# Vision tower: the tokenizer's first two layers as one product over raw pixels, q formed transposed and x (Wv W_out) joined to k in linear attention

## The chip, the cores and the metric

One core of a Trainium2 chip. The time is device microseconds from a run without the profiler, the median of three runs. The core has TensorE (PE, with weight loads PEld beside it), VectorE (DVE), ScalarE (ACT), GpSimd (POOL) and SyncE (SP), which issues most transfers. All data are float32.

## The reference

Four images of 3 x 224 x 224 are cut into 8 x 8 patches, 784 tokens of 192 pixel values for each image, and pass through two layers of a tower.

```python
# tokenizer
tokens = layernorm(patches, ln1_g, ln1_b)              # over 192
tokens = tokens @ W1 + b1                              # 192 -> 256
tokens = layernorm(tokens, ln2_g, ln2_b)
tokens = concatenate([tokens, tokens, tokens], axis=1) # three equal copies
h1 = silu(layernorm(tokens @ Wp1 + bp1, lnp_g, lnp_b))
return h1 @ Wp2 + bp2
```

```python
# linear attention of layer 1, on the normed rows x
q, k, v = split(x @ W_qkv + b_qkv, 3)
q = q - mean(q);  k = k - mean(k)                      # over the 256 channels
q2, k2 = q * q, k * k
k2 = l2_normalize(k2 / (sum(k2) + 1e-7), axis=-2)      # over the tokens
q2 = l2_normalize(q2 / (sum(q2) + 1e-7), axis=-1)      # over the channels
t2 = (q2 @ (k2.T @ v)) / sqrt(N)
return (v + t2) @ W_out + b_out
```

Between the two, layer 0 has attention over the four images (norm, q, k, v, a gate) and a mixture of six experts, of which each token takes two. After the linear attention layer 1 has a feed-forward of a shared part and four experts. Each part's result is added to the rows. The three copies of the tokens are equal, so the kernel computes one of them and writes each row of the result three times.

## The kernel before

Tokens are handled in tiles of 112 rows, 7 to an image, 28 in all; a group is four tiles. `h` (L258) holds all rows of the residual stream in SBUF. The stages, in order of time:

- Start. `img` (four transfers on SP and ACT, L211) has one image in 28 partitions, `W1`, `ln1` (the norm's scale and shift) and the rest follow. `turn_patches(k)` (L342) turns four patch columns at a time on PE into `pT`, pixels on partitions, and ACT copies them out (L352). `bn_stats` of the pixels (L443) is on DVE. After five of seven column groups `first_layer` (L357) folds the norm's scale and the subtraction of the mean into `W1`, and puts the rows into the order of `pT` with `perm` (L390). `patch_scales` (L397) makes one factor per token (`rtok`). DVE and PE follow the order of the program here (`manual_schedule`).
- Tokenizer, three steps deep (`tokenize`, L499). For group g: `pw1`, 256 wide, over `pT` (L508), the factor and `b1` by DVE (L466), statistics (L470), root on ACT (L474), `xn` on DVE (L482). Then for group g-1: turn of `xn` (L297), scale and shift of the second norm on ACT (L492), `pwp1` with `Wp1` (L514), bias, statistics and `xn` again. Then for group g-2: turn, Silu on ACT (L492), `pwp2` (L522) and the bias into `h` (L461). A planner orders the instructions of each engine.
- Keys and values of layer 0 (`keys_values`, L1016), between the last two steps of the tokenizer and after them, in an order by hand. Keys of all images have to be there before the first image's attention ends.
- Attention of layer 0, routing, and the experts over 30 blocks of 256 rows, which are scattered to `xrows` and fetched from `yrows` with indirect DMAs on POOL (L901, L1369). Both arrays are filled with zeros at the start (L253). In the expert stage DVE and SP are ordered by hand; `centred_weights` (L577) takes the mean out of the columns of q and k in `Wqkv`.
- Linear attention, in eight units of four or three tiles (`units`, L1349; the loop is L1705). Per unit: `x_t` turns the normed rows, `q_k` (L1558) forms q and k, 512 wide, DVE adds the bias (L1578), ACT squares q, k and q again with sums (L1582, L1583), `scales` (L1591) scales both (L1606 on ACT, L1607 on DVE), `q_t` turns q (L1628). Per image `k_x` forms k^T x (L1648) and `kv_out` multiplies with Wv W_out, which `layer1_weights` (L593) made in unit 1. `rows_out` (L1682) adds x (Wv W_out) (L1689) and q kvo (L1694) in PSUM and DVE adds the sum to `h` (L1700). The rows of the experts of the unit after are added in `stats_one` (L1377), inside `q_k`. The planner orders all engines here.
- Feed-forward of layer 1 in seven groups, with its router `gate` (L1506).

PSUM has seven banks in turn (`ps_tile`) and one bank of its own for small products (`psum_s`, L70), one user at a time.

Of the kernel before, what the change touches and what calls it, by code (L numbers as in the profile page):

```python
# [27 lines left out]
P = 128  # L28
# [32 lines left out]
def tile_vit_tower(ctx: ExitStack, tc: tile.TileContext, a: dict, out: bass.AP):  # L61
# [45 lines left out]
    for n in (E0, E1):  # L107
# [4 lines left out]
    allones = const.tile([TT, TT], F32, tag="allones", name="allones")  # L112
# [3 lines left out]
        out=before, in_=allones, compare_op=ALU.is_ge, fill=0.0, base=-1,  # L116
# [36 lines left out]
    for key, name in (  # L153
        ("ln2_g", "L0_tok_ln2_g"), ("ln2_b", "L0_tok_ln2_b"), ("lnp_g", "L0_tok_lnp_g"),
        ("lnp_b", "L0_tok_lnp_b"), ("gamma", "L0_attn_gamma"), ("beta", "L0_attn_beta"),
        ("bg", "L0_attn_bg"), ("router_b1", "L0_ffn_router_b1"), ("sb1", "L1_ffn_sb1"),
        ("sb2", "L1_ffn_sb2"),
    ):
        want(key, a[name].rearrange("(r p) -> r p", p=P), a[name].shape[0] // P)
# [5 lines left out]
    nrows = sum(k for _, k, _ in plan)  # L165
    stage = const.tile([nrows, P], F32, tag="stage", name="stage")
# [37 lines left out]
    tok = ctx.enter_context(ExitStack())  # L204
    tokp = tok.enter_context(tc.tile_pool(name="tok", bufs=1))
    WID = HP * PATCH
    CY = CH * PATCH
    img = tokp.tile([TT, 32, WID], F32, tag="img", name="img")
    for b in range(NI):
        eng = nc.scalar if b % 2 else nc.sync  # L210
        eng.dma_start(  # L211
            out=img[b * HP : (b + 1) * HP, :CY, :].rearrange("h (c p) w -> h c (p w)", c=CH),
            in_=a["x"][b].rearrange("c (h p) w -> h c (p w)", p=PATCH),
        )
    ln1 = tokp.tile([2, PD], F32, tag="ln1", name="ln1")
    nc.scalar.dma_start(out=ln1[:1], in_=a["L0_tok_ln1_g"].unsqueeze(0))
    nc.scalar.dma_start(out=ln1[1:], in_=a["L0_tok_ln1_b"].unsqueeze(0))
    W1 = tokp.tile([KP, 2, D], F32, tag="W1", name="W1")
    nc.sync.dma_start(out=W1, in_=a["L0_tok_W1"].rearrange("(s p) n -> p s n", p=KP))
# [8 lines left out]
    b1 = spread(tokp, "b1", a["L0_tok_b1"])  # L228
    Wp1 = tokw.tile([P, 2, D], F32, tag="Wp1", name="Wp1", bufs=1)
    nc.sync.dma_start(out=Wp1, in_=a["L0_tok_Wp1"].rearrange("(c p) n -> p c n", p=P))  # L230
    bp1 = tokw.tile([TT, D], F32, tag="bp1", name="bp1", bufs=1)
    nc.gpsimd.dma_start(out=bp1, in_=a["L0_tok_bp1"].partition_broadcast(TT))
# [106 lines left out]

    pT = tokp.tile([P, 2, NI * HP, HP], F32, tag="pT", name="pT")  # L340

# [15 lines left out]
    def first_layer():  # L357

        gbT = tokp.tile([KP, 2, 2], F32, tag="gbT", name="gbT")
        pt = ps_tile("pgb")  # L360
        for i in range(2):
# [3 lines left out]
        nc.vector.tensor_copy(gbT.rearrange("p i k -> p (i k)"), pt[:KP, :4])  # L365
        bb = tokp.tile([KP, 2, TT], F32, tag="bb", name="bb")
        W1g = tokp.tile([KP, 2, D], F32, tag="W1g", name="W1g")
        for i in range(2):
            nc.vector.tensor_copy(bb[:, i, :], gbT[:, i, 1:2].to_broadcast([KP, TT]))
            nc.vector.tensor_scalar(  # L370
                W1g[:, i, :], W1[:, i, :], gbT[:, i, 0:1], None, ALU.mult
            )
        pw = ps_tile("pbw")[:TT, :D]
        for i in range(2):
            nc.tensor.matmul(pw, bb[:, i, :], W1[:, i, :], start=(i == 0), stop=(i == 1))
        pm = ps_tile("pw1m")[:KP, :D]
        for i in range(2):
            nc.tensor.matmul(
                pm, allones[:KP, :KP], W1g[:, i, :], start=(i == 0), stop=(i == 1)
            )  # L380
        nc.vector.tensor_tensor(b1, pw, b1, ALU.add)
        for i in range(2):
            nc.vector.scalar_tensor_tensor(
                W1g[:, i, :], pm, -1.0 / PD, W1g[:, i, :], ALU.mult, ALU.add
            )
        Wc = tokp.tile([P, 2, D], F32, tag="Wc", name="Wc")
        pp = ps_tile("pwc").rearrange("p (i d) -> p i d", i=2)
        for i in range(2):
            for half in range(2):
                nc.tensor.matmul(  # L390
                    pp[:, i, :], perm[:, half, i].rearrange("p g k -> p (g k)"),
                    W1g[:, half, :], start=(half == 0), stop=(half == 1),
                )
        nc.vector.tensor_copy(Wc, pp)
        return Wc

    def patch_scales(st):  # L397


        d = tokp.tile([TT, HP], F32, tag="pd", name="pd")  # L400
        v = tokp.tile([TT, HP], F32, tag="pv", name="pv")
# [4 lines left out]
        nc.scalar.activation(v, v, AF.Sqrt, bias=eps[:TT], scale=1.0 / PD)  # L406
        nc.vector.reciprocal(v, v)
# [3 lines left out]
            rr, v.unsqueeze(1).to_broadcast([TT, 4, HP]),  # L411
# [4 lines left out]
        rtok = tokp.tile([TT, NT], F32, tag="rtok", name="rtok")  # L416
        nc.vector.tensor_copy(rtok, pr)
        return rtok
# [4 lines left out]
    perm = tokp.tile([KP, 2, 2, 4, 32], F32, tag="perm", name="perm")  # L423
    pst = tokp.tile([TT, HP, 6], F32, tag="pst", name="pst")
    with tc.manual_schedule(engines={mybir.EngineType.DVE, mybir.EngineType.PE}):
        nc.vector.memset(perm, 0.0)
# [3 lines left out]
        for half in range(2):  # L430
            for i in range(2):
# [5 lines left out]
                )  # L437
        for k in range(HP // GT):
            if k == 5:
                W1g = first_layer()  # L440
            turn_patches(k)
            for w in range(k * GT, (k + 1) * GT):
                nc.vector.bn_stats(pst[:, w, :], img[:, :CY, w * PATCH : (w + 1) * PATCH])  # L443
        rtok = patch_scales(pst)
# [7 lines left out]
    def added(pm_of, dst, bias, stats, scale=None):  # L452

        st = mv = None
        if stats:
            st = small.tile([TT, GT, 6], F32, tag="st", name="st")
            mv = small.tile([TT, GT, 2], F32, tag="mv", name="mv")
        for two in halves(range(GT)):
            pm = pm_of(two)
            if scale is None:  # L460
                nc.vector.tensor_tensor(  # L461
                    dst[:, two[0] : two[0] + 2, :], pm, over(bias, 2), ALU.add
                )
            else:
                for i, j in enumerate(two):
                    nc.vector.scalar_tensor_tensor(  # L466
                        dst[:, j, :], pm[:, i, :], scale(j), bias, ALU.mult, ALU.add
                    )
            for j in two if stats else ():
                nc.vector.bn_stats(st[:, j, :], dst[:, j, :])  # L470
                nc.vector.bn_aggr(mv[:, j, :], st[:, j, :])
        if stats:
            r = small.tile([TT, GT], F32, tag="rstd", name="rstd")
            nc.scalar.activation(r, mv[:, :, 1], AF.Sqrt, bias=eps[:TT])  # L474
            return mv, r

    def rows_of(y, stats):
        mv, r = stats
# [9 lines left out]
    def turned_rows(xn, func, g, b):  # L488
        xT = tokw.tile([P, 2, GN], F32, tag=f"xT{g}", name=f"xT{g}")

        def put(c, pt):
            nc.scalar.activation(xT[:, c, :], pt, func, scale=col(g, c), bias=col(b, c))  # L492
# [4 lines left out]
    second, third = {}, {}  # L497

    def tokenize(g):  # L499
        if 1 <= g <= len(groups):  # L500
# [1351 lines left out]
```

## Time and profile before

| | us |
|---|---|
| time, three runs | 812.31, 815.91, 816.70 (median 815.91) |
| profiled execution | 849.85 |
| its span, first to last instruction | 848.1 |
| images landed, first patch statistics | 17.2 |
| first product of the tokenizer (L508) | 39.3 |
| second group of keys and values (L1016) starts turning | 150.4 |
| last product of the expert stage ends | about 517 |
| linear attention's last output row (L1694) ends | about 703 |

The profiled execution is one run under the profiler. Stretches of time below are in us from the start of its span. "PEclk" is the share of its full clock that TensorE was granted. A stage's limit is read from the engine that is busy there, not from shares of the whole span.

### The profile page before, as it was taken

The numbers are of one execution on the slowest core, as the hardware profiler recorded it, in microseconds if no ns is written. First come the engines' busy times: TensorE is split into PE (matmuls) and PEld (weight loads), VectorE is DVE, ScalarE is ACT, GpSimd is POOL, SyncE is SP. The second block draws the span as 40 slices with busy tenths as digits, with TensorE's granted clock in tenths as the row PEclk, the third lists the DMA queues.
The fourth block names the chain that finished last, engine by engine and source line by source line (L and its number), as shares of the span: only waits on it lengthen the run. The fifth ranks groups of instructions, "written<-read, shape, count | busy, mean of one in ns | idle before, by whom it ended". The sixth has DMA issues, their size and how long they took to land. (4 is left out here: it accounts for less than half of the span.)

```text
span 848.1 us, 11129 instructions
## 1 busy us (share of the span) xinstructions
PE 746.0 (88%) x3669; PEld 525.4 (62%) x3669; DVE 515.1 (61%) x1619; ACT 318.2 (38%) x758; POOL 129.3 (15%) x151
## 2 busy tenths in 40 slices
PE   2879988999788788799999999348999999999996
PEld 2758765555465466678878885335767675555553
DVE  4369886585787874346445655358995745544441
ACT  1333535455547573242222323323564612222221
POOL 5100000000024605430030022744000000000000
PEclk9999999999999988799999999759999999999999
DMA  8999990000001293332342224311000001333333
GB/s 197 360 421 419 419 384 0 1 0 1 1 22 55 82 367 95 103 127 75 100 131 88 94 88 137 93 52 55 1 2 0 1 3 27 100 101 101 99 100 100
DMA packets 58286, 97.52 MB, mean 115 GB/s; under 512 B 14590, under 2 KB 48564, under 8 KB 53364
## 3 DMA queue, kind: packets, MB, share of 16 engines
q1 hardware_dynamic: 51100, 80.78, 27.7%
q0 software_dynamic: 6224, 14.13, 5.8%
q10 hardware_dynamic: 904, 1.89, 0.9%
q8 instruction: 29, 0.48, 0.2%
q14 instruction: 29, 0.24, 0.1%
HBM read 31.04 MB, written 65.74 MB: 114 GB/s over the span
## 5 line engine op out<-in xcount | busy, mean ns | idle before, releaser
L901 POOL DMA_INDIRECT xrows<-xn,pos x56 | 59.9, 1070 | 282.4 <-ACT kq L665 233.2
L1369 POOL DMA_INDIRECT ys<-yrows,pos x56 | 54.3, 969 | 163.5 <-DMA yrows<-yb 134.0
L1173 PE MATMUL pb<-xTb,own 128*128 128x256 f32 x240 | 60.3, 396 | 7.0 <-DVE hb L1181 2.1
L1190 PE MATMUL pyb<-own,hb 128*128 128x256 f32 x240 | 59.4, 392 | 4.4 <-ACT hb L1179 4.4
L1173 PE MATMUL pb<-hb,own 128*128 128x256 f32 x240 | 58.8, 388 | 0.3 <-DVE hb L1181 0.3
L1179 ACT ACTIVATE hb<-pb,own 128x256 f32<-128x256 f32 x74 | 34.7, 473 | 61.7 <-PE pb L1173 42.1
L1173 PEld LDWEIGHTS pb<-xTb,own 128*128 128x128 f32 x240 | 45.5, 198 | 16.7 <-ACT xTb L1163 3.8
L1190 PEld LDWEIGHTS pyb<-own,hb 128*128 128x128 f32 x240 | 46.9, 197 | 12.0 <-ACT hb L1179 5.2
L297 PE MATMUL pt<-ident,xn 112*128 112x112 f32 x280 | 42.2, 281 | 12.4 <-DVE xn L482 6.9
L1574 PE MATMUL pqk<-Wqkv,lxT 128*112 128x512 f32 x112 | 50.0, 595 | 0.5 <-ACT lxT L81 0.5
L297 PEld LDWEIGHTS pt<-ident,xn 112*128 112x128 f32 x280 | 32.4, 148 | 26.4 <-issue 9.1
L1173 PEld LDWEIGHTS pb<-hb,own 128*128 128x128 f32 x240 | 44.5, 195 | 6.2 <-DVE hb L1181 0.7
L1196 DVE TENSOR_TENSOR yb<-pyb,eb 128x512 f32<-128x512 f32 x30 | 20.7, 691 | 45.5 <-PE pyb L1190 35.3
L306 PE MATMUL pe<-xT,eW 128*128 128x448 f32 x112 | 45.2, 546 | 0.0
L1648 PE MATMUL pukx<-xa,uk 112*128 112x258 f32 x112 | 29.0, 415 | 18.5 <-ACT uk L1606 18.5
L1163 ACT COPY xTb<-ptb 128x512 f32<-128x512 f32 x30 | 17.5, 583 | 73.8 <-PE ptb L1159 65.2
L1181 DVE TENSOR_SCALAR hb<-pb,own 128x256 f32<-128x256 f32 x46 | 22.2, 482 | 30.9 <-PE pb L1173 29.6
L1648 PEld LDWEIGHTS pukx<-xa,uk 112*128 112x128 f32 x112 | 22.7, 208 | 22.3 <-issue 18.8
L317 PE MATMUL pwo<-Wo,oT 128*112 128x256 f32 x112 | 29.0, 413 | 7.6 <-DVE oT L730 6.7
L1574 PEld LDWEIGHTS pqk<-Wqkv,lxT 128*112 128x112 f32 x112 | 19.2, 177 | 25.2 <-issue 22.7
L690 DVE SCALAR_TENSOR_TENSOR prod<-kq 128x784 f32<-128x784 f32 x32 | 30.4, 971 | 7.2 <-ACT kq L665 5.0
L1582 ACT ACTIVATE qk<-qk 112x256 f32<-112x256 f32 x56 | 22.8, 407 | 28.1 <-DVE qk L1578 23.8
(339 smaller groups left out, 1525.4 us busy)
## 6 DMA issues: line engine op xcount, KB each, us to landing
xrows<-nothing SPq DMA_DIRECT2D x19, 1024.0 KB
yrows<-nothing SPq DMA_DIRECT2D x19, 1024.0 KB
out_dram<-h SPq DMA_DIRECT2D x26, 336.0 KB
xb<-xrows SPq DMA_DIRECT2D x30, 256.0 KB
yrows<-yb SPq DMA_DIRECT2D x30, 256.0 KB
ew<-in_L_ffn_expert_w_dram SPq DMA_DIRECT2D x6, 768.0 KB
wb<-wd SPq DMA_DIRECT2D x28, 112.0 KB
img<-in_x_dram ACTq DMA_DIRECT2D x2, 588.0 KB
```

What stands on the lines that cost most here:

```text
L297: nc.tensor.transpose(pt[:, j * TT : (j + 1) * TT], xn[:, j, c * P : (c + 1) * P], ident[:TT, :TT])
L306: nc.tensor.matmul(pm[: wcols.stop - wcols.start, :n], w[:, c, wcols], xT(c), start=(c == 0), stop=(c == chunks - 1),)
L317: nc.tensor.matmul(pm[:, i, :], xT(c, t), w[:, c, :], start=(c == 0), stop=(c == chunks - 1))
L690: nc.vector.scalar_tensor_tensor(prod, qTs[s][:, o, :], 1.0, kT[:, o, t * SEQ : (t + 1) * SEQ], ALU.mult, ALU.mult, accum_out=atts[s][:, o ...
L901: put = nc.gpsimd.indirect_dma_start(out=xrows[:, :], out_offset=bass.IndirectOffsetOnAxis(ap=pos[:, k, t0 + j : t0 + j + 1], axis=0), in_ ...
L1173: nc.tensor.matmul(pm, wm[:, c, o * P : (o + 1) * P], src[:, c, :], start=(c == 0), stop=(c == 1),)
L1179: nc.scalar.activation(dst[:, o, :], pm, AF.Relu, bias=b)
L1190: nc.tensor.matmul(pm[:, t, :], src[:, c, t * P : (t + 1) * P], wm[:, c, :], start=(c == 0), stop=(c == 1),)
L1369: got = nc.gpsimd.indirect_dma_start(out=y[:, j, k, :], out_offset=None, in_=yrows[:, :], in_offset=bass.IndirectOffsetOnAxis(ap=pos[:, k, ...
L1574: nc.tensor.matmul(pqk, xT[:, c, cut(j, 1)], Wqkv[:, c, : 2 * D], start=(c == 0), stop=(c == 1),)
L1582: nc.scalar.activation(half, half, AF.Square, accum_out=ss[:, j, i : i + 1])
L1648: nc.tensor.matmul(pg, uks[u][:, k, c * P : (c + 1) * P], xas[u % 4][:, k, : D + 2], start=(j == 0), stop=(j == TPI - 1),)
```

## The change

- Start: the vectors, `W1` and `Wp1` are fetched ahead of the images; `b1` is one row instead of a copy per partition; `Wp1` and `bp1` move to the pool of the first stage. Row 24 of `img` in its last column now takes each patch's standard deviation (ACT's root, written in place), so that it is turned with the pixels and multiplies `b1` in the product.
- `first_layers` takes the place of `first_layer`, ahead of the first patches. It also folds the second norm's scale, shift and mean into `Wp1` and forms the product of both layers, so that `Wall` is 512 wide: the first layer's result in its first half (only its variance is used) and both layers' in the second.
- `first_rows` takes the place of the first two steps of the tokenizer: one 512-wide product per tile, statistics of its first half straight from PSUM, a copy of the second half by ACT, then factor, bias, statistics and `xn`. The turn between the layers and its activation go. The tokenizer is two steps deep.
- Linear attention: `q_of` forms q transposed (weights stationary), squares it on the way out of PSUM; the sums for its scale come from `norms`, with products of 32 columns and a turn in `psum_s`; the scale is applied in `rows_out`. `k_of` forms k and x (Wv W_out) in one 512-wide product, except in unit 0, and adds the latter to `h` at once; `rows_out` then has only q kvo. W_v in `Wqkv` is overwritten by Wv W_out. `layer1_weights` is called before unit 1.

```diff
+    nc.sync.dma_start(out=ln1[:1], in_=a["L0_tok_ln1_g"].unsqueeze(0))
+    nc.scalar.dma_start(out=ln2[:2], in_=a["L0_tok_ln2_g"].rearrange("(r p) -> r p", p=P))
+    nc.sync.dma_start(out=ln1[1:], in_=a["L0_tok_ln1_b"].unsqueeze(0))
+    nc.scalar.dma_start(out=ln2[2:], in_=a["L0_tok_ln2_b"].rearrange("(r p) -> r p", p=P))
+    nc.sync.dma_start(out=W1, in_=a["L0_tok_W1"].rearrange("(s p) n -> p s n", p=KP))
+    nc.scalar.dma_start(out=b1, in_=a["L0_tok_b1"].unsqueeze(0))
+    nc.scalar.dma_start(out=Wp1, in_=a["L0_tok_Wp1"].rearrange("(c p) n -> p c n", p=P))
     for b in range(NI):
         eng = nc.scalar if b % 2 else nc.sync
         eng.dma_start(
...
+    def without_mean(w, n, dim):
+        pm = ps_tile("pmean")[:n, :D]
+        for i in range(2):
+            nc.tensor.matmul(pm, allones[:n, :n], w[:, i, :], start=(i == 0), stop=(i == 1))
+        for i in range(2):
+            nc.vector.scalar_tensor_tensor(
+                w[:, i, :], pm, -1.0 / dim, w[:, i, :], ALU.mult, ALU.add
+            )
+    def first_layers():
...
+        for i in range(2):
+            nc.vector.tensor_scalar(W1g[:, i, :], W1[:, i, :], g1(i), None, ALU.mult)
+        without_mean(W1g, KP, PD)
...
+        nc.vector.tensor_tensor(b1, pw, b1, ALU.add)
...
+        nc.tensor.matmul(pp[:, 1, :], srow, b1, start=False, stop=True)
+        Wall = tokp.tile([P, 2, 2 * D], F32, tag="Wall", name="Wall")
+        nc.vector.tensor_copy(Wall[:, :, :D], pp)
+        for c in range(2):
+            nc.vector.tensor_scalar(W2[:, c, :], Wp1[:, c, :], g2(c), None, ALU.mult)
...
+        without_mean(W2, P, D)
...
+        nc.scalar.copy(WcT, pt)
...
+        nc.vector.tensor_tensor(bp1, pw, bp1, ALU.add)
+        pp = ps_tile("pw2").rearrange("p (i d) -> p i d", i=2)
+        for i in range(2):
+            for f in range(2):
+                nc.tensor.matmul(
+                    pp[:, i, :], WcT[:, f, i * P : (i + 1) * P], W2[:, f, :],
+                    start=(f == 0), stop=(f == 1),
+                )
+        nc.vector.tensor_copy(Wall[:, :, D:], pp)
+        return Wall
+    def patch_stds(k):
+        w0 = k * GT
+        for w in range(w0, w0 + GT):
+            nc.vector.bn_stats(pst[:, w, :], img[:, :CY, w * PATCH : (w + 1) * PATCH])
...
+        nc.vector.tensor_tensor(d, st[:, :, 1], st[:, :, 4], ALU.subtract)
+        nc.vector.tensor_tensor(v, st[:, :, 2], st[:, :, 5], ALU.add)
+        nc.vector.scalar_tensor_tensor(d, d, PD / 4.0, d, ALU.mult, ALU.mult)
+        nc.vector.tensor_tensor(v, v, d, ALU.add)
+        nc.scalar.activation(
+            img[:, CY, w0 * PATCH : (w0 + GT) * PATCH].rearrange("q (w x) -> q w x", x=PATCH)[
+                :, :, PATCH - 1
+            ],
+            v, AF.Sqrt, bias=eps[:TT], scale=1.0 / PD,
+        )
...
+        Wall = first_layers()
         for k in range(HP // GT):
-            if k == 5:
-                W1g = first_layer()
+            patch_stds(k)
             turn_patches(k)
...
+    def first_rows(g):
...
+        for j in range(GT):
+            pm = ps_tile("pw1")[:TT]
+            for c in range(2):
+                nc.tensor.matmul(
+                    pm, pTf[:, c, cut(t0 + j, 1)], Wall[:, c, :], start=(c == 0), stop=(c == 1)
+                )
+            nc.scalar.copy(y[:, j, :], pm[:, D:])
+            nc.vector.bn_stats(st[:, j, :], pm[:, :D])
+            nc.vector.bn_aggr(mv[:, j, :], st[:, j, :])
...
+        for j in range(GT):
+            nc.vector.scalar_tensor_tensor(
+                y[:, j, :], y[:, j, :], r[:, j : j + 1], bp1, ALU.mult, ALU.add
+            )
+            nc.vector.bn_stats(st[:, j, :], y[:, j, :])
+            nc.vector.bn_aggr(mv[:, j, :], st[:, j, :])
...
     def tokenize(g):
+        if g < len(groups):
+            normed[g] = first_rows(g)
         if 1 <= g <= len(groups):
+            third[g - 1] = turned_rows(normed.pop(g - 1))
...
+    def k_of(u):
...
+                if lw:
+                    pk = ps_tile("pk")[:TT]
+                    for c in range(2):
+                        nc.tensor.matmul(
+                            pk, xT[:, c, cut(j, 1)], Wqkv[:, c, D:], start=(c == 0), stop=(c == 1)
+                        )
+                    nc.vector.tensor_tensor(kr[:, j, :], pk[:, :D], bqkv[:, D : 2 * D], ALU.add)
+                    ht = h[:, b * TPI + j0 + j, :]
+                    nc.vector.tensor_tensor(ht, pk[:, D:], ht, ALU.add)
+                nc.scalar.activation(
+                    kr[:, j, :], kr[:, j, :], AF.Square, accum_out=ss[:, j : j + 1]
+                )
...
+    def q_of(u):
...
+        for o in range(2):
+            pq = mm_t(
+                n * TT, Wqkv, slice(o * P, (o + 1) * P), lambda c: xTs[u][:, c, : n * TT], "pq1"
+            )
+            nc.scalar.activation(qT[:, o, : n * TT], pq, AF.Square, bias=bq[:, o : o + 1])
+        nc.scalar.activation(q4[:, :, : n * TT], qT[:, :, : n * TT], AF.Square)
+    def norms(u):
...
+        for c in range(2):
+            for j in range(n):
+                nc.tensor.matmul(
+                    pg[32 * j : 32 * (j + 1), :], ones32, q4[:, c, cut(j, 1)],
+                    start=(c == 0), stop=(c == 1),
+                )
...
+        nc.scalar.copy(qn, pg)
+        pr = psum_s.tile([P, 512], F32, tag="pss", name="pqn")[:TT, :n]
+        nc.tensor.matmul(
+            pr, qn, ident.rearrange("p (j e) -> p j e", e=32)[: 32 * n, :n, 0],
+            start=True, stop=True,
+        )
...
     def rows_out(u):
...
+            pq = mm_rows(two, lambda c, j: qT[:, c, cut(j, 1)], kvo, "pqo")
+            for i, j in enumerate(two):
+                nc.vector.scalar_tensor_tensor(
+                    ht[:, i, :], pq[:, i, :], r[:, j : j + 1], ht[:, i, :], ALU.mult, ALU.add
+                )
...
+            k_of(0)
+            q_of(0)
             squares[0] = scales(0)
             fold(0, squares.pop(0))
+            lw.extend(layer1_weights(bvs))
+            Wvo, bvo = lw[:2]
...
         if u < len(units):
-            q_k(u, 0, 2)
+            k_of(u)
+            norms(u - 1)
```

## The prediction

> **What bounds the kernel now.** I read three views: the page (who is busy, when), busy time by stage, and the chain of work that ended last. First the page:
>
> ```profile
> span 848.1 us, 11129 instructions
> PE 746.0 (88%) x3669; PEld 525.4 (62%) x3669; DVE 515.1 (61%) x1619; ACT 318.2 (38%) x758; POOL 129.3 (15%) x151
> PE   2879988999788788799999999348999999999996
> DVE  4369886585787874346445655358995745544441
> PEclk9999999999999988799999999759999999999999
> DMA  8999990000001293332342224311000001333333
> ```
>
> One slice is 21.2 us. PE (TensorE) is full almost everywhere. It is not full at the start (slices 0 to 3) and in slices 25 and 26, where its clock falls too. DMA is full until 125 us, but with the zero fill of `xrows` and `yrows`, which nothing near it waits for. So I cut the two stages that the change touches:
>
> ```profile
> core 0: us, PE busy (x) PEld busy (x) DVE busy (x) ACT busy (x) POOL busy (x), PEclk, DMA share, GB/s
> 28.00:33.30 5.30, 4.15 (x25) 2.92 (x26) 2.20 (x8) 0.53 (x1) 0.00 (x0) 1.00 1.00 420
> 39.30:60.00 20.70, 15.97 (x73) 11.91 (x73) 14.76 (x52) 3.70 (x8) 0.00 (x0) 0.91 1.01 423
> 60.00:122.00 62.00, 60.65 (x308) 49.55 (x307) 50.91 (x166) 27.72 (x38) 0.00 (x0) 0.97 1.01 419
> 122.00:150.40 28.40, 22.89 (x96) 15.52 (x95) 18.11 (x58) 12.40 (x20) 0.00 (x0) 0.94 0.12 51
> 531.00:575.00 44.00, 18.16 (x68) 14.42 (x69) 19.81 (x61) 11.84 (x41) 26.45 (x28) 0.69 0.26 74
> 575.00:640.00 65.00, 63.73 (x268) 42.30 (x267) 61.75 (x178) 34.41 (x131) 6.98 (x7) 1.00 0.05 15
> 640.00:703.00 63.00, 62.42 (x297) 45.68 (x296) 34.74 (x113) 24.03 (x78) 0.00 (x0) 1.00 0.01 2
> ```
>
> The reader is to see: the tokenizer's steady part (60 to 122) is PE's, with DVE at 82%; its filling (39.3 to 60) and its end (122 to 150.4) each leave PE idle for about 5 us. Linear attention is PE's from 575 on. In 531 to 575 no engine is full. There ACT and DVE stand still for 5 to 11 us at a time with nothing that the profile shows to wait for:
>
> ```profile
> DVE ss L1597 <- issue: 10.8, 1, 10.8
> ACT lqT L81 <- remote: 9.0, 1, 9.0
> ```
>
> These stalls come to some 30 us, and the profiled execution (849.85 us) is 34 us over the median of the timed runs (815.91). I take them to be mostly the profiled execution's own. The last view, the chain, has these lines in linear attention:
>
> ```profile
> 593.03 5.40 PE pqk L1574 x12
> 598.43 0.77 PE pt L297 x8
> 599.20 0.87 PE pout L1689 x4
> 600.07 0.86 PE pout L1694 x4
> ```
>
> Matmul follows matmul, so in this stage a microsecond of PE work is a microsecond of time. The chain gives prices: a 512-wide matmul record 5.15/12 = 0.429 us (628.95), 256 wide 0.216, 448 wide 3.02/8 = 0.377, a turned 112x112 tile 0.77/8 = 0.096. PE time goes with columns: twice 256 costs as much as once 512.
>
> **What the Trainium skill says.** "TensorE: Matmul & The Clock Gate", section "What's actually happening": the clock is halved after an idle window of about 3.4 us and comes back after a busy one. The trace agrees: PEclk is 0.91 in the filling and 0.69 in 531 to 575. "TensorEngine Tiling (Array Packing)", section "Key Properties": separate column groups run at the same time. The trace agrees: the router's 32-column matmuls (L1513) take 0.52 us for 16, 0.033 each, where a 112-wide one alone takes 0.096. "ScalarE: Activation LUTs", section "What ACT_TABLE_LOAD costs": 1283 ns a load; the trace has 1283 (L492, L474). Square, Copy and Sqrt change without a load in 580 to 670, so the new Squares add none.
>
> **The change, part by part.**
>
> *Transfers at the start.* `W1`, `Wp1` and the vectors now go ahead of the four images. In the trace the ninth transfer of SP and ACT (`Wp2`, 10.01) waits for the first one to land; with the new order `img` 1 to 3 wait that way for vectors of under 1 KB, about 2 us. `W1` and `Wp1` are 448 KB; the images moved 2.35 MB in about 14 us, 168 GB/s, so 448 KB are 2.7 us. The images land at 20 instead of 17.2 us.
>
> *`first_layers`.* It was 5.3 us between patches 5 and 6 (window 28 to 33.3). It now stands ahead of all patches on PE and DVE, in an order fixed by hand, and is about twice as long. I add it from 7.4 us (DVE done with `perm`) on: W1g 1.0; mean 4 records at half clock 1.7; `pbw` and `b1` 2.1; `pwc` 10 records 3.5; its copy 0.7; W2 and `bb` 1.0; mean, STT 1.7; four transposes and ACT's copy 1.6; `pbw2` with `bp1` in its shadow; `pw2` 8 records 2.0; last copy 0.7. That ends at 23 us, 3 after the images: the transfers hide 12.6 of it. Without that cover it would all be on the path.
>
> *Patches.* Per group of four columns DVE has 4 statistics of 0.26 and four small operations of 0.17, 1.73 us; PE has 1.54 (two 0.77); ACT 2 copies and a root, 1.4. DVE sets 7 x 1.73 = 12.1; then 0.6 root, 1.6 turn, 0.8 copy: the first product starts at 23.1 + 15.4 = 38.5 us, where it was 39.34. The long wait for `patch_scales` (36.5 to 39.3) is gone, but the images and `first_layers` eat it.
>
> *Tokenizer.* Per group of four tiles PE had 3 x 16 x 0.216 + 16 x 0.096 = 11.9 (measured 12.5 from group to group: 73.29, 85.81, 98.32, 110.83). Now 16 x 0.429 + 16 x 0.216 + 8 x 0.096 = 11.1. The product is not halved, only a turn falls: 0.8 us. With the same 0.4 to 0.6 of gaps it is 11.5, so seven groups save 7 us. DVE had 11.2; now per tile statistics from PSUM 0.40+0.15, STT 0.44, statistics 0.37+0.15, `xn` 0.345, `h` 0.35, and 0.6 per group: 9.4. ACT loses two activations of 0.72 per group and gains four copies of 0.4. The pipeline is one stage shorter. After the last product of a group DVE still needs 8.1 us (0.9, root 0.8, 3.8, root 0.9, 1.4, handovers) until `xn`; PE has pw1 of the next group (6.9) beside it. Laid out: pw1(0) 38.5, pw1(1) 45.4, stall 2.7, pw1(2) 55.8, stall 0.8, group 3 done at 79.3, then 11.5 each: group 6 at 113.8 (before: 121.9). The end: `xn`(6) at 118.4, turn, Wp2(5), keys of group 0 at 126, Wp2(6), and `keys_values(1)` starts at 138 instead of 150.4. That is -12.4 us for the front, and all behind it moves as one, since every image's keys are needed.
>
> *Expert stage.* Two tiny matmuls and three DVE copies: +0.5.
>
> *Linear attention.* PE per image (7 tiles) before: qk 28 x 0.429 = 12.0, turns of q 1.35, two outputs 12.1. After: k and x(Wv W_out) in one, 12.0; q transposed 8 x 0.377 + 8 x 0.283 = 5.3; norms 1.2 (bounded by the 0.033 and 0.096 above: 0.7 to 2); one output 6.0. 24.5 for 25.4: -0.9 an image, -3.6. DVE per tile loses a 0.29 scaling of q and 0.15 of copies and gains 0.1 (two adds of 256 instead of one of 512) and 0.14 (an STT per tile for an add per two). ACT drops a Square and two reads of sums a tile, gains 0.5. In 518 to 537 DVE is what holds `WvT` back (5.8 us PE idle before L607); it has about 2 us less to do there: -2. Against that `k_of(1)` now waits for Wv W_out (turn, copy, product, copy: 4.4 us, less 3 of `q_of(0)` beside it): +1.5. `norms` holds the single bank of `psum_s` over PE, ACT, PE; the router's chain (L1513, L1520) has the same form and PE works between its parts, so I take +1 for all, with 0 and 20 as ends. Sum -3.
>
> *Total:* -12.4 + 0.5 - 3 = -15: the profiled execution 850 becomes 835, the median 816 becomes 801. The savings lie where PE is the bound or the front's latency is, so I carry them over to the median unchanged.
>
> **The rivals.**
> - *The front's order is hidden wholly.* If `first_layers` ends before the images land, pw1 starts at 35.5, and if scheduling fills the stalls of filling (3.5) and end, 7 more us go: 793. For it: PE and DVE are idle until 17 us. Against: the chain is serial at half clock.
> - *DVE's latency takes the tokenizer.* Two norms now stand in one step; if a group takes 13 us by its 8 us tail, 7 x 1.5 us go back: 811. For it: DVE at 82% before. Against: its work falls by 16%, and PE has 4.2 us of other work plus 6.9 of the next product.
> - *Slower: the bank of `norms`.* PE works in order; if the second small product stands right behind the first, it waits for ACT's copy, behind the last Square of `k_of`: about 2.9 us (0.7 DVE add, 0.6 Square and read, 0.3 copy, handovers) x 8 units = 23 us: 801 + 23 - 1 = 823. It decides from 1.9 us a unit on (15/8). Against: the router's chain in the trace.
>
> **How the numbers follow.** Forecast 0.56 (795 to 807), first rival 0.17, second 0.15, slower 0.12. A change of 0.5%, 4 us, is about what can be told from none. Faster: all of the first two and 0.11 of the second rival, 0.84; same 0.04; slower 0.12. Range 788 to 815: it holds forecast and both faster rivals with the bounds of transfers and norms; outside are the slower one and a little below, some 0.15 to 0.2.
>
> **What would show it.** The first `pw1` at 38 to 39 us; 11.5 us from group to group; `keys_values(1)` about 12 us earlier; 112 records of 512 x 0.43 in pw1; PE between the two `norms` products busy; the rows of output in the tail half as long. I'm wrong if images land after 23 us, if a group takes 12.5, or if PE idles at `pqn`.

## The result and the profile after

The change made the kernel slower. The median went from 814.11 us (810.64 to 816.70, four runs) to 823.93 us (821.51 to 826.82, four runs); the ratio is 1.0138, 95% interval 1.0103 to 1.0173, so about 10 us more where 15 us less were forecast. The profiled execution took 826.82 us, the slowest of the four. From the page of the profile after, the head and two rows of its 40 slices (20.6 us each):

```profile
span 825.1 us, 10886 instructions
PE 748.1 (91%) x3568; PEld 500.3 (61%) x3568; DVE 496.7 (60%) x1621; ACT 327.6 (40%) x708; POOL 131.0 (16%) x148
PE   5779996999789878987999999698999999999996
PEclk9889997999999988998999999888999999999999
```

There are 101 matmul records fewer than before, yet PE is busy 748.1 us (735.7 in the second profile of before, below). Two places are to be seen: PE is still not full in slices 0 to 2 (counted from 0), and TensorE's clock is at 0.8 in slices 25 to 27, the start of linear attention. The profile before can't be set beside this one as it stands, because its execution was 34 us longer than the timed runs. A second profile of the same kernel (run e0) is the one to compare with:

```profile
span 812.5 us, 11129 instructions
PE   0879998899798887999999999699999999999996
PEclk9999999999999988999999999899999999999999
```

The hole of slices 25 and 26 has shrunk to one slice at 0.6, and its clock is 0.8 there. The marks below are read from PE's timelines (a tile's number, as in pw1, is left out in the trace):

| us from the start of the span | before (e0) | after | change up to here |
|---|---|---|---|
| first product of the tokenizer (pw1) | 41.5 | 50.9 | +9.3 |
| first block of the experts turned (ptb) | 315.6 | 311.3 | -4.3 |
| last block of the experts turned | 494.2 | 497.4 | +3.3 |
| first product of linear attention | 505.2 | 508.5 | +3.3 |
| first expert product of the feed-forward (pe) | 668.1 | 680.4 | +12.3 |
| last matmul ends | 805.8 | 818.1 | +12.3 |

So three stages differ from the forecast: the start of the kernel (the tokenizer itself is faster), the experts by +7.6 us, linear attention by +9.0 us. In e0 the images landed 1.9 us later than in the first profile (turns from 19.1 us, not 17.2); two other traces with the old start have pw1 at 39.3 and 39.5, so the start loses 9 to 11.5 us.

**The start.** PE's timeline of the kernel after, while the pixels are turned (start, length, line, operation, number of records; in brackets the idle time before them and what ended it):

```profile
24.85 1.22 PE L356 MATMUL ptp<-ident,img 112*32 112x112 f32 x38
28.15 3.77 PE L356 MATMUL ptp<-ident,img 112*32 112x112 f32 x136 [2.07 <-ACT img L452]
34.82 6.19 PE L356 MATMUL ptp<-ident,img 112*32 112x112 f32 x128 [2.91 <-issue]
42.12 3.32 PE L356 MATMUL ptp<-ident,img 112*32 112x112 f32 x128 [1.10 <-issue]
48.86 1.28 PE L356 MATMUL ptp<-ident,img 112*32 112x112 f32 x18 [3.42 <-issue]
```

The 448 records take 25.3 us. 2.07 us are a wait for the first root. 7.4 us are put down to "issue": nothing that the profile shows was waited for. Each of these gaps comes 128 records after the last (38 + 136 = 174, then 302, 430), wherever the data stand. And 128 records took 6.19 us at one place and 3.32 at the next, so the clock was halved meanwhile (the mean granted in 33.3 to 41 us was 0.56).

**The experts.** The timeline of PE around the new product pbq:

```profile
376.24 1.89 PE L1229 MATMUL pb<-hb,own 128*128 128x256 f32 x8
382.82 1.01 PE L640 MATMUL pbq<-ones,bqkv 1*128 1x1 f32 x4 [4.69 <-DVE bqkv L635]
383.76 3.78 PE L1229 MATMUL pb<-xTb,own 128*128 128x256 f32 x8
387.34 2.72 PE L1246 MATMUL pyb<-own,hb 128*128 128x256 f32 x8
389.89 0.60 PE L1215 MATMUL ptb<-ident,xb 128*128 128x128 f32 x4
```

Four records of one column stand in PE's order ahead of a block of the experts. PE reaches them at 378.1 and stands until DVE has centred the bias (the last step of `centred_weights`). Then the eight records of `pb` take 3.78 us instead of 1.89. From the start of one turned block (ptb, 375.81 us) to the next (389.89) it is 14.08 us, for a usual block 5.62.

**Linear attention.** The whole stage: its length, busy time and records of PE, PEld, DVE, ACT and POOL, then the mean clock, the share of the transfer engines and GB/s; first the kernel before (e0), then the changed one:

```profile
505.24:668.10 162.86, 154.55 (x671) 107.08 (x669) 123.55 (x369) 76.47 (x277) 42.27 (x42) 0.98 0.11 33
```

```profile
508.51:680.39 171.88, 158.96 (x710) 102.95 (x709) 117.35 (x373) 66.19 (x190) 42.36 (x42) 0.94 0.11 31
```

PE's idle time rose from 8.3 to 12.9 us, and its busy time rose too, by 4.4 us, at a mean clock of 0.94 instead of 0.98. DVE and ACT have less to do, as forecast; it did not help. A part of the busy time is the clock, in two stretches:

```profile
547.81 3.78 PE L1763 MATMUL pkvo<-Wqkv,gT 128*128 128x256 f32 x8 [0.68 <-ACT gT L1754]
574.62 8.14 PE L1641 MATMUL pk<-Wqkv,lxT 128*112 128x512 f32 x12 [1.75 <-ACT lxT L81]
```

In e2's trace (below), which runs the same code, these records take 1.99 and 5.40 us.

### The profile page after: what moved, and what is told of

The parts are those of the page before. It is cut to its first block, busy times and chain, and to the rows that moved or that the text cites. A ratio compares the mean times of both kernels' runs of the same rounds, so it can differ in the third digit from the quotient of the medians.

```text
span 825.1 us, 10886 instructions
## 1 busy us (share of the span) xinstructions
PE 748.1 (91%) x3568; PEld 500.3 (61%) x3568; DVE 496.7 (60%) x1621; ACT 327.6 (40%) x708; POOL 131.0 (16%) x148
## 5 line engine op out<-in xcount | busy, mean ns | idle before, releaser
L1430 POOL DMA_INDIRECT ys<-yrows,pos x56 | 57.1, 1019 | 149.8 <-DMA yrows<-yb 133.6
L1229 PE MATMUL pb<-hb,own 128*128 128x256 f32 x240 | 56.8, 380 | 0.0
L1229 PEld LDWEIGHTS pb<-xTb,own 128*128 128x128 f32 x240 | 45.7, 199 | 12.3 <-issue 1.7
L517 PE MATMUL pw<-Wall,pT 128*112 128x512 f32 x112 | 51.1, 611 | 0.0
L1641 PE MATMUL pk<-Wqkv,lxT 128*112 128x512 f32 x96 | 45.4, 626 | 3.7 <-ACT lxT L81 2.0
L300 PE MATMUL pt<-ident,xn 112*128 112x112 f32 x224 | 34.5, 286 | 12.4 <-DVE xn L540 6.8
L1252 DVE TENSOR_TENSOR yb<-pyb,eb 128x512 f32<-128x512 f32 x30 | 20.7, 692 | 41.2 <-PE pyb L1246 40.8
L300 PEld LDWEIGHTS pt<-ident,xn 112*128 112x128 f32 x224 | 26.9, 151 | 26.5 <-ACT xn L834 9.4
L517 PEld LDWEIGHTS pw<-Wall,pT 128*112 128x112 f32 x112 | 20.2, 183 | 26.3 <-issue 22.9
L1641 PEld LDWEIGHTS pk<-Wqkv,lxT 128*112 128x112 f32 x96 | 17.7, 187 | 27.3 <-issue 20.6
L309 PEld LDWEIGHTS pe<-xT,eW 128*128 128x128 f32 x112 | 20.2, 190 | 20.9 <-issue 20.9
## 6 DMA issues: line engine op xcount, KB each, us to landing
ew<-in_L_ffn_expert_w_dram SPq DMA_DIRECT2D x6, 768.0 KB, 11.5
```

The source lines that it names most:

```text
L300: nc.tensor.transpose(pt[:, j * TT : (j + 1) * TT], xn[:, j, c * P : (c + 1) * P], ident[:TT, :TT])
L309: nc.tensor.matmul(pm[: wcols.stop - wcols.start, :n], w[:, c, wcols], xT(c), start=(c == 0), stop=(c == chunks - 1),)
L517: nc.tensor.matmul(pm, pTf[:, c, cut(t0 + j, 1)], Wall[:, c, :], start=(c == 0), stop=(c == 1))
L1229: nc.tensor.matmul(pm, wm[:, c, o * P : (o + 1) * P], src[:, c, :], start=(c == 0), stop=(c == 1),)
L1430: got = nc.gpsimd.indirect_dma_start(out=y[:, j, k, :], out_offset=None, in_=yrows[:, :], in_offset=bass.IndirectOffsetOnAxis(ap=pos[:, k, ...
L1641: nc.tensor.matmul(pk, xT[:, c, cut(j, 1)], Wqkv[:, c, D:], start=(c == 0), stop=(c == 1))
```

## The experiments

Times are medians; ratios are against the kernel before on the same chip, with their 95% intervals. The changed kernel had 823.93 us (1.0138) at first and 820.56 us (1.0107) in a second set, e10, so what an edit of it gains is given as a span between these two ratios. Four chips were used: the kernel before took 812.07 us on that of e0 to e2, 813.94 on that of e3 to e6, 850.98 on that of e7 to e9 and 812.27 on that of e10 to e13. The changed kernel itself was not run on the second and the third, so spans for edits tried there lean on the ratio carrying over.

### The two halves alone

e0 is the kernel before, unchanged. e1 takes the part of the change up to the tokenizer, e2 the part in the experts and in linear attention.

> The kernel before, unchanged, for a second profile of it. Theory A (the 30 us of idle in 531 to 575 and the 6 us at 338 to 344 of its first profile belong to that one execution): the span is 809 to 816 us, linear attention lasts about 155 us from its first product to its last, and the expert stage is some 6 us shorter than in the first profile. Theory B (the idle is the program's own): the span is again about 848.

> The new start and tokenizer with the linear attention of the kernel before. Theory A (start-up loses 11.5 us, the tokenizer gains 13.4): 1 to 3 us faster than before. Theory B (the change's loss of 10 us lies in the start and tokenizer, and what follows only passes it on): 8 to 12 us slower. My prediction's step was 12.4 us faster.

> The old start and tokenizer with the new linear attention. Theory A (a wait of about 4.7 us at the product pbq in the expert stage, and some 8 us lost in the start of linear attention): 10 to 14 us slower than before. Theory B (loss in the start of the kernel): 1 to 3 us faster, as predicted (2.5).

| | us | ratio |
|---|---|---|
| e0 | 814.28 (one run, span 812.5) | |
| e1 | 809.09 | 0.9944 (0.9922 to 0.9966) |
| e2 | 826.95 | 1.0172 (1.0141 to 1.0202) |

e0: on this chip the 30 us of idle are gone, so they do not belong to the program alone. Linear attention lasts 162.9 us in e0; I had expected 155. e1 and e2 add up to +1.2%, the change's own +1.1 to +1.4%: so within the noise the halves don't disturb each other. By the ratios the new tokenizer is worth 4.5 us (3.0 by the medians), a third of the forecast 12.4; the other half costs 14 us.

The profiled execution of e2 is the fastest of its six. Its linear attention takes 166.4 us with PE busy 153.90, the changed kernel's 171.9 with 158.96, for the same code:

```profile
509.12:675.56 166.44, 153.90 (x711) 100.20 (x709) 116.45 (x373) 66.21 (x190) 42.75 (x42) 0.98 0.12 32
```

The runs of e2 list spans of 820.0 us at a mean clock of 0.969 and of 824.6 to 828.5 at 0.957 to 0.963. So in some executions about 5 us more go to a halved clock: in five of e2's six, and in the changed kernel's profile, which has both stretches shown above where e2's has neither. What brings them on is not shown: the same idle times, at most 0.7 us ahead of the first stretch and 1.75 ahead of the second, stand in e2's trace without them. PE idles 12.5 us in this stage and 8.3 in e0's. Here is how it idles at its start, in the timeline of e2, and, in the last two lines, at the turn from unit 2 to unit 3:

```profile
515.58 0.60 PE L611 MATMUL pwv<-ident,Wqkv 128*128 128x128 f32 x4
520.01 0.97 PE L1631 MATMUL pq<-q,ones 128*32 128x112 f32 x16 [3.83 <-ACT q L1621]
522.50 3.78 PE L620 MATMUL pwvo<-Wout,WvT 128*128 128x256 f32 x8 [1.52 <-ACT WvT L615]
528.70 1.54 PE L1595 MATMUL pk<-Wqkv,lxT 128*112 128x512 f32 x3 [1.44 <-ACT Wqkv L624]
570.17 0.59 PE L1631 MATMUL pq<-q,ones 128*32 128x112 f32 x16 [1.38 <-ACT q L1621]
572.52 5.40 PE L1595 MATMUL pk<-Wqkv,lxT 128*112 128x512 f32 x12 [1.75 <-ACT lxT L81]
```

The kernel before (e0) has one wait at its start, and none over 0.24 us at the turn to unit 3:

```profile
524.01 3.78 PE L607 MATMUL pwvo<-Wout,WvT 128*128 128x256 f32 x8 [6.15 <-DVE WvT L602]
```

At the start e2 has three waits in a row, all for ACT: the squares of q for the first product of `norms`, the copy of WvT, the copy of Wv W_out that unit 1's product needs. Together they are 6.8 us, 0.6 more than the one wait in e0; most of the 4.2 us of new idle time is the 3.1 us at the turn to unit 3. In the changed kernel's trace ACT's first `uk` waits there 3.06 us for a scale from DVE, DVE being held by rows that are still being fetched, and the second Square of q, its fourth power and the copy of WvT stand behind that `uk` in ACT's order.

### The three losses, each mended by itself

e3 takes the two products pbq and DVE's copy out of `centred_weights`:

```diff
+    def q_bias():
+        pb = ps_tile("pbq")
...
         if u == 0:
             fetch(3)
+            q_bias()
             x_t(1)
```

e4 holds the zero fill of `xrows` and `yrows` back, by a column of the zeros that is made from the last turned pixels (the loop goes from its old place):

```diff
     pTf = pT.rearrange("p c q w -> p c (q w)")
+    nc.gpsimd.tensor_scalar(nothing[:, :1], pTf[:, 1, NI * HP * HP - 1 :], 0.0, None, ALU.mult)
+    for r in range(0, XROWS, 8 * P):
...
```

e5 calls `layer1_weights` first and q before k in unit 0; e6 makes all three edits:

```diff
-            k_of(0)
             q_of(0)
-            squares[0] = scales(0)
-            fold(0, squares.pop(0))
             lw.extend(layer1_weights(bvs))
             Wvo, bvo = lw[:2]
+            k_of(0)
+            squares[0] = scales(0)
+            fold(0, squares.pop(0))
```

> The changed kernel with the two products pbq (bias of q as a column) taken out of the expert stage and put at the start of linear attention. Theory A (PE stands in its fixed order before pbq for 4.7 us until DVE has centred the bias, and its clock is halved for some 5 us after it): 6 to 8 us faster than the changed kernel, 815 to 818 us, no PE idle at that place above 2 us, and the next block's 8 records take 1.9 us instead of 3.8. Theory B (the wait is DVE's work on Wqkv, which some product needs at once wherever pbq stands): within 1.5 us of the changed kernel.

> The changed kernel with the zero fill of xrows and yrows held back until the last turned pixels are copied (about 40 us), so that the transfers stand idle while the pixels are turned. Theory A (PE's idle of 2.9, 1.1 and 3.4 us between runs of 128 records, which the profile puts down to nothing, is its instructions coming in late behind the fill, and the halved clock follows from it): these idles fall under 0.7 us, pw1 starts 7 to 10 us earlier (41 to 44 us), the kernel is 5 to 9 us faster than the changed one (815 to 819). Theory B (ACT's order of roots and pT copies sets the pace): pw1 at 49 to 51 us, time as the changed kernel. A cost of its own: the fill ends some 15 us later, about 140 us, ahead of the first scatter.

> The changed kernel with layer1_weights called ahead of k_of(0) and q_of(0) ahead of both, so that unit 0 too has its 512-wide product. Theory A (the start of linear attention loses by waits in a row: q's squares, copy of WvT, Wv W_out): PE idle before the first pq4, pwvo and k_of(1), 7.3 us together, falls under 3.5, and the halved clock after it goes: 4 to 8 us faster than the changed kernel (816 to 820). Theory B (the stage is held by the fetched rows ys and DVE, so waits only move to unit 2): within 2 us of the changed kernel.

> The changed kernel with the three edits together. If the three losses are separate they add up: 17 to 22 us faster than the changed kernel, 802 to 808 us, which is also faster than the kernel before (812). If the waits only move, 812 or more.

| | us | ratio |
|---|---|---|
| e3 | 817.38 | 1.0050 (1.0027 to 1.0073) |
| e4 | 829.20 | 1.0214 (1.0168 to 1.0260) |
| e5 | 817.59 | 1.0052 (1.0022 to 1.0083) |
| e6 | 819.62 | 1.0104 (1.0057 to 1.0150) |

e3 gains 4.6 to 7.1 us over the changed kernel (0.57 to 0.88%), as theory A has it; against e10's ratio alone the two intervals just overlap, but the traces agree: from the first turned block to linear attention it is 190.9 us, 197.2 in the changed kernel. The block of the timeline above now takes 5.62 us, and the next one 7.15, since DVE's centring still holds it for 1.5; it did so in the kernel before (7.0). So the price of pbq was 8.46 - 1.5, 7 us, of which 2.7 is the halved clock.

e5 gains 4.5 to 7.0 us. The waits at the start are 0.76 us where they were 6.8 in e2, but a new one of 5.15 has come, at pqn of unit 0, as the timeline of e5 shows:

```profile
511.37 1.99 PE L666 MATMUL pwvo<-Wout,WvT 128*128 128x256 f32 x8 [0.76 <-ACT WvT L661]
514.06 12.18 PE L1641 MATMUL pk<-Wqkv,lxT 128*112 128x512 f32 x28
532.68 0.53 PE L1684 MATMUL pqn<-ident,qn 128*112 128x4 f32 x2 [5.15 <-ACT qn L1682]
```

This is the mechanism of my slower rival (the copy between the two products of `norms` queued behind ACT's Squares). It came with e5's order; in the changed kernel itself PE never waits more than 0.4 us at pqn. So the idle time of the stage fell by only 2.2 us, from 12.9 to 10.7; in these two traces the other 4.7 us are PE's busy time (154.2 us for 159.0), at a mean clock of 0.97 instead of 0.94.

e4 is a miss in time and a hit in its place. In its timeline the same 448 records take 15.2 us, and pw1 starts at 40.18 instead of 50.85:

```profile
24.58 1.21 PE L349 MATMUL ptp<-ident,img 112*32 112x112 f32 x38
27.88 10.47 PE L349 MATMUL ptp<-ident,img 112*32 112x112 f32 x392 [2.08 <-ACT img L445]
39.01 0.73 PE L349 MATMUL ptp<-ident,img 112*32 112x112 f32 x18 [0.67 <-issue]
```

ACT's order of roots and copies is as before, so theory B falls; 40.18 us is what DVE's seven groups allow (worked out below). What the fill does to PE is seen in the answer about transfers for 24 to 41 us, first of the changed kernel, then of e4 (queue, packets, MB, share of the 16 transfer engines):

```profile
q1 hardware_dynamic: 914, 6.73, 94.6%
...
q8 instruction: 2, 0.03, 0.6%
```

```profile
q0 software_dynamic: 38, 0.01, 4.1%
q8 instruction: 4, 0.07, 1.8%
```

With the fill the transfer engines are full and two packets start on q8, the queue of instructions, in 17 us; without it four. By their number these packets are PE's: 28 of 16,384 bytes in the whole run, for 3568 matmul and 3568 weight-load records, 255 to a packet, so one for 128 matmuls with their loads. In the changed kernel's trace they start at 32.57, 39.69 and 46.66 us and take 0.9 us each; PE goes on at 34.82, 42.12 and 48.86, each time 1.3 to 1.6 us after a packet is through. In e4 they start at 28.86, 32.59 and 36.11, 3.5 to 3.7 us apart instead of 7, and of the gaps 0.67 us is left. So PE ran dry of instructions, and the fill made them late. Where PE takes few instructions the same fill does no harm: from 62 to 122 us, at 420 GB/s, the changed kernel has 215 matmul records and PE is busy throughout.

But e4 is slower than the changed kernel, by 0.8 to 1.1%, because the gain was lost further on. Two lines of ACT's timeline of e4:

```profile
120.42 1.34 ACT L551 ACTIVATE xTt<-pt,cols 128x448 f32<-128x448 f32 x2
142.57 1.34 ACT L1078 ACTIVATE mT<-pt,cols 128x448 f32<-128x448 f32 x2 [20.80 <-DMA yrows<-nothing]
```

`mT` takes over memory of the tile of zeros, and the late fill was still reading it. The first keys started at 143.3 us, after 139.0 in the changed kernel. This is what the late fill costs and what e4's expectation put at nothing. e6, expected at 802 to 808 us, is a miss too: its first keys start at 143.6 us, so it carries the same loss.

### The fill from a tile of its own

e7 is e4 with the zeros in a small tile that nothing takes over. e8 adds e3's and e5's edits. e9 also puts `patch_stds` of the first two column groups inside `first_layers`, and `norms(0)` ahead of `k_of(0)`.

```diff
-    nothing = tokp.tile([P, 8 * D], F32, tag="nothing", name="nothing")
+    nothing = const.tile([P, D], F32, tag="nothing", name="nothing")
...
-                in_=nothing[:, : n * D],
+                in_=nothing.unsqueeze(1).to_broadcast([P, n, D]),
```

> As e4_fill_late, but the zeros are read from a small tile of their own (256 columns, read eight times per row of the transfer) whose memory nothing takes over. Theory A (in e4 the late fill was paid for by mT, whose copy waited 20.8 us for the fill to stop reading memory it takes over): the first keys start at 126 to 131 us instead of 143, pw1 still at 40 to 41 us, and the kernel is 7 to 10 us faster than the changed one (814 to 817). Theory B (the transfers themselves hold the keys): as e4, 827 to 830.

> e7's fill, e3's pbq and e5's order together. If the three losses are separate: 824 - 9 - 6.5 - 6.3, 800 to 804 us, and 8 to 12 us faster than the kernel before. If the front's gain is lost at a later wait again: 811 or more.

> e8 with two more moves: the statistics and roots of the first two column groups stand inside first_layers, and norms(0) stands ahead of k_of(0). Theory A (PE waits 2.1 us for the first root; and about 5 us at pqn of unit 0, whose copy is queued on ACT behind the Squares of k): pw1 at 36 to 38 us, the idle before the first pqn under 1 us, 5 to 8 us faster than e8. Theory B (DVE sets the turns and the fetched rows set unit 0): within 2 us of e8.

| | us | ratio |
|---|---|---|
| e7 | 854.94 | 1.0055 (1.0030 to 1.0081) |
| e8 | 838.01 | 0.9845 (0.9809 to 0.9880) |
| e9 | 840.88 | 0.9871 (0.9838 to 0.9903) |

On the chip of these three the kernel before takes 850.98 us, so only the ratios can be used, and with care: e7's kernel has another ratio on the next chip (e11 below). Their traces have long idle times of ACT and DVE (in e8 at 320 to 345 and 528 to 550 us) for which the profile shows nothing on this core that ended them, while POOL issues indirect transfers, like those of the first profile of before. In e7 the first keys start at 125.5 us, as theory A says, and pw1 at 39.9. e8 is the first version of the whole change that beats the kernel before (e1, the tokenizer alone, did so by 0.6%), by 1.5%, 13 us there, where 8 to 12 were expected. In e9 pw1 starts at 37.1 us and the wait for the first root is gone, but it isn't faster than e8, and PE still idles 2.8 us ahead of the first pqn. On this chip such unexplained idle times lie over the start of linear attention, so e9 against e8 stays undecided.

### All on one chip

e10 is the changed kernel again, e11 is e7's kernel, e13 is e9's. e12 has e9's front and the linear attention of the kernel before; its tile of zeros lies in the pool of layer 0's weights (`wts`).

> The changed kernel, unchanged, on the same chip as the three that follow. It should stand at 1.010 to 1.017 of the kernel before, 821 to 827 us on a chip on which the kernel before takes 812 us.

> e7's kernel beside the changed one. The front is 14 us earlier in e7's trace than in the changed kernel's; if all of it stays to the end, 12 to 14 us faster than e10; if the later stages give a part back, 6 to 9 us faster.

> e9's front (late fill from its own tile, early statistics) with the linear attention of the kernel before. Theory A (tokenizer and start are worth 12 us and more once PE's instructions come in time): 14 to 19 us faster than the kernel before. Theory B (the front's gain is lost at the keys): within 6 us of the kernel before.

> e9's kernel beside e12: it differs from e12 in having the new linear attention, with its waits taken out. Theory A (without the waits the new linear attention is worth the 1.4 to 3.6 us of PE work that it saves): 2 to 6 us faster than e12. Theory B (PE's work hardly falls, 0.65 us in the trace of e2): within 2 us of e12.

| | us | ratio |
|---|---|---|
| before | 812.27 | |
| e10 | 820.56 | 1.0107 (1.0063 to 1.0151) |
| e11 | 812.49 | 0.9985 (0.9966 to 1.0004) |
| e12 | 793.86 | 0.9781 (0.9739 to 0.9823) |
| e13 | 795.86 | 0.9801 (0.9758 to 0.9843) |

e11 is 8.1 us faster than e10 by the medians, and level with the kernel before. By the two traces it is 12.0 ahead at pw1, 12.5 at the first expert block and 11.5 at the last matmul, so in these two executions the front's gain is kept once nothing waits for the fill. They lie above their medians, e10's by 6.4 us and e11's by 2.9, so the medians' 8.1 us, which the expectation takes for a part given back, stays the measure of the gain.

e12 is 18.4 us faster than the kernel before: the tokenizer's part of the change, with the fill moved and the first statistics early, is worth more than the 12.4 us forecast. pw1 starts at 36.55 us there. What moving the fill would do for the kernel before alone was not tried; its gaps before turns come to 0.2 (e0) to 0.6 us (e2).

e13 is 2.0 us slower than e12, so theory B holds: the new linear attention is worth nothing even with PE's idle time brought down to the old one's (7.9 us in the stage, 7.4 in e12). In the timeline of e13 the start now runs through, and `norms` costs PE 0.6 us and no wait; other waits remain behind it, 2.7 us for ACT's `uk` and 2.6 at the turn to unit 3:

```profile
491.89 1.99 PE L672 MATMUL pwvo<-Wout,WvT 128*128 128x256 f32 x8 [0.76 <-ACT WvT L667]
494.68 0.59 PE L1683 MATMUL pq<-q,ones 128*32 128x112 f32 x16
496.15 0.27 PE L1690 MATMUL pqn<-ident,qn 128*112 128x4 f32 x2
```

Yet the stage takes 161.75 us, and 160.99 in e12, with PE busy 153.87 and 153.54. First e12, then e13:

```profile
485.80:646.79 160.99, 153.54 (x671) 106.44 (x669) 123.59 (x369) 76.49 (x277) 42.58 (x42) 0.98 0.11 33
```

```profile
487.50:649.25 161.75, 153.87 (x694) 98.18 (x693) 115.61 (x377) 66.85 (x190) 41.97 (x42) 0.98 0.11 33
```

The rest of the 2 us lies in the experts, which take 192.9 us from the first turned block to the first product of linear attention in e13 and 191.4 in e12.

## Why the prediction was wrong

**"The first product starts at 38.5"**, in the step on patches, is the first that failed: 50.85. What went into it was near: DVE took 1.65 us a group (1.73 forecast), the images had landed by 20.7 us (in e9 DVE reads them then without a wait), though `first_layers` ended at 25.6, not 23. (Its listed parts give 23.4 us, and those of the patches 15.1, not 15.4; the two slips cancel.) The sum took PE's turns as hidden beside DVE. It left out what else runs then. In the first profile of the kernel before, transfers fall almost idle at 26 us and the fill gets going at 26.7; 320 of the 448 records had run by 28.0. In e0 and e2 the gaps marked "issue" are 0.2 and 0.6 us. Beside the fill e0's packets of instructions are 6.5 us apart too, but PE had only 128 turns left. With `first_layers` ahead of them nearly all 448 run beside the fill. The price was 10.7 us (e4). The rest of the miss, 1.7 us, is the later end of `first_layers`: 25.6 and seven groups of 1.65 and the forecast's 3.0 for root, turn and copy make 40.2, where e4 has 40.18. I had called the fill something "which nothing near it waits for"; it was in the way all the same.

**The tokenizer's own steps held.** A group takes 11.1 us (11.5 forecast, 12.5 before); from pw1 to the second group of keys it is 97.7 us where the forecast had 138 - 38.5 = 99.5. The rival that let DVE's latency set the groups is refuted. None of the three signs that the prediction named for being wrong came: the images landed before 23 us, a group did not take 12.5, and PE did not idle at pqn (0.4 us at most). What failed lay outside them.

**"Two tiny matmuls and three DVE copies: +0.5"** was the second failure. It priced the instructions and not their place: PE's order, and DVE's 4.2 us of centring, which until then lay nearly all beside PE's work. +7 us by the block's timeline, 6.3 by the stage's length, and gone in e3.

**"Sum -3" in linear attention** was the third: e2's trace has +3.6 us, of which 4.2 are more idle time and -0.6 PE's work. "PE -3.6" was mis-sized: from unit to unit of the same kind in the steady part an image takes 35.43 us in e2 for 35.79 in e0, -0.36 where -0.9 stood, and over the stage PE's busy time fell by 0.65 us. The parts measured, each from its start to the next one's: the transposed q 5.4 us an image (5.3 forecast), norms 1.3 (1.2), one output 6.0 (6.0). The removed turns and output are 1.3 + 6.0. That makes -0.6; the rest, 0.2, I can't place. "Startup -2, Wvo wait +1.5" took the waits one by one. In the run the start waits 6.8 us in three steps of ACT where it had waited 6.15 for DVE, so nothing was saved there, and the turn to unit 3 waits 3.1 us, 0.2 before, where the sum had at most the +1 for `norms`. The two further stretches at half clock in the changed kernel's profile, 5.1 us of PE's busy time, make up nearly all of what its +9.0 is above e2's +3.6; their cause is open.

**The slower rival** did not happen in the changed kernel. It had the right sign, and 823 for its number, which the measured 823.93 meets by luck: the bank of `norms`, on which it rests, cost nothing of the kind there.

**"I carry them over to the median unchanged"** was sound in that the 30 us of stall are not in e0 and did not return in the changed kernel's profile. It hid that without them the old start of linear attention left less idle to save, 8.3 us in the whole stage.

## What to carry to other kernels

A product of a few columns costs its place in the order of its engine, not its length: ask what the engine that feeds it is doing then, and put it where PE waits anyway. An engine's idle time that ends in "issue" at even counts of instructions is a reason to look at what the transfer queues are doing, and a fill that nothing waits for can still be moved; but then look for what takes over its memory. Where several small steps of a start stand in one engine's order, add them up in a row, and set the sum against the wait that they replace.

## What the hardware showed that was not expected

- PE stood 1.1 to 3.4 us after each 128 matmul records while the zero fill ran (398 GB/s in 24 to 41 us), and hardly (0.67 us at most) without it. Its packets of instructions, 16,384 bytes each, came 7 us apart beside the fill and 3.5 to 3.7 without it, and PE went on 1.3 to 1.6 us after each.
- Idle of 4.69 us on PE was followed by about 6 us at half clock (eight records of 256 columns in 3.78 us, then in 2.72, where 1.89 is usual), so its price there was 2.7 us on top of the idle itself. "TensorE: Matmul & The Clock Gate", section "What's actually happening", in the Trainium skill says that an idle window halves the clock, and the trace agrees; the prediction had read it only as a description of the stages and not as a price on each new wait. Not every stretch at half clock in these traces has such a wait ahead of it: that at 547.8 us in the changed kernel follows idle times of 0.7 us at most.
- One of four chips takes 851 us for the kernel before, where the other three take 812 to 814. On it the traces show long idle times of ACT and DVE that nothing on this core ends, beside POOL's indirect transfers. The first profile of the kernel before, 849.85 us, lies within that chip's nine runs (848.96 to 853.01) and has such idle times, so its 30 us of stall may be a chip's and not one execution's own; the record does not say on which chip it ran.
